# Four graph layers on one core: adjacency and weight products in the array form that TensorE is in, and layer 0's last products by row halves

## The chip, the core and the metric

The kernel runs on one core of a Trainium2 chip. The metric is the time of one execution in microseconds (us) on the device; the runs before the change took 2094.66, 2096.2 and 2099.83 us, a median of 2096.2. A profile is a record of one execution: each instruction of the engines TensorE (PE, with its weight loads as PEld), VectorE (DVE), ScalarE (ACT), GpSimd (POOL) and SyncE (SP), with start and duration.

## What is computed

Eight batches of 2048 nodes with 64 channels go through four layers, each followed by a residual sum and a layer norm. All data is float32.

```python
# layer 0: A is adj (2048 x 2048); emb is 2048 x 16, weight 16 x 3 x 64 x 64
w = einsum('nd,dkio->nkio', emb, weight); b = emb @ bias
x_g = stack([x, A @ x, 2 * A @ (A @ x) - x])
x = layernorm(x + einsum('bnki,nkio->bno', x_g, w) + b)
# layer 1: attention; a is 128 x 1
e = leaky_relu((x @ a[:64]) + (x @ a[64:]).T, 0.2)
att = softmax(where(adj > 0.5, e, -9e15))
x = layernorm(x + elu(att @ x))
# layer 2
x = layernorm(x + (adj + I) @ (x @ W.T + b2) / rowsum(adj + I))
# layer 3: row 0 replaced by a given value, then three steps
for _ in range(3):
    v = relu(concat(v, adj @ v) @ W1.T + b1) @ W2.T + b3
x = layernorm(x + v)
```

## The kernel before

**Data.** The eight batches are taken as four pairs (p = 0 to 3); a pair fills 128 columns (2 batches of 64 channels). SX[p] holds a pair's x as 16 tiles of 128 nodes by 128 columns. SA, SB and SH are three more slots of that size. A chunk (c = 0 to 3) is 512 nodes, four tiles.

**Adjacency products.** `sweep` (L1087) multiplies one or two such sources with the transposed adjacency, which streams from DRAM in tiles of 128 x 2 x 512 (512 KB) over SP's queue into a ring of six. For each chunk, 16 calls (L1106) add up into a PSUM bank `acc` of 128 columns by 512 nodes: weights are a source tile (128 x 128), moving are 512 nodes of adjacency. `sweeps` (L1359) lists all in a fixed order: A x for pairs 0 and 1, then per pair A (A x) together with A x of a later pair, layer 2 and the three steps of layer 3 of pairs 0 and 1, layer 2 of pairs 2 and 3, and last layer 3 of pairs 2 and 3 jointly (`joint_layer3`, L1184, with products at L1219 and L1203). Each whole sweep for one pair has 64 calls, 128 records in the trace, since a call leaves two. Layer 2 of pair 3 waits for `("x2", 3)`, the end of layer 1 for that pair (L1383).

**Layer 0.** `y1_chunk` (L527) takes A x out of PSUM, keeps it node-wise in SA or SB (after transposes, L539) and also writes it to DRAM as `y1_cols`. `stacks` (L559) builds, per chunk, a stack `xgT` of 128 rows for each batch of the pair: 64 rows of x (transposed at L572, two copies) and 64 rows of y1 (one DMA from `y1_cols`). `second_pass` (L584) then makes, for each tile t and each half h of the 16 weight sets, `yp` of 128 nodes x 2 batches x 512: two calls with the 128-row stack and the weights `w01`, one for each batch, and two calls of 64 rows with y2 and `wk2`, in the two row halves of the array (L609). The order is stack first for h = 0, y2 first for h = 1. `add_terms` (L622) weighs the 16 sets by the embedding and adds them into SX on ScalarE and VectorE (L633, L636, L645, L647); `first_norm` (L654) adds the embedding's bias `eb` (L658, on VectorE, from SBUF) and normalises. `embedding_bias` (L376) makes `eb` near the start.

**Layer 1.** `layer1` (L668) transposes x and makes the scores' two halves (L690), `scores` (L709) finds row maxima with the masks (L740), `weights` (L807) makes a tile of exponentials e for both batches: VectorE (L818), ScalarE (L826), VectorE (L831), ScalarE (L834). Two such tiles together go to TensorE at L845: eight calls with 64 columns of weights each, for the two batches in the two column halves of the array, adding up in `po`. Only then is the ring of four e buffers given back. `finish` (L862) ends layer 1 with small products at L879 and a layer norm whose last step is L518.

**Small products.** Also with 128 x 128 weights: L991 (layer 2's weights), L1041 and L1061 (layer 3's), and the seeds of `acc` at L1095. Transposes are at L539, L572, L680, L793 and L1026.

**What sets the order.** The program is scheduled while it is written. Each piece of work is a generator that yields the engine it needs next and what it waits for; `Plan` keeps a clock per engine and in `go` (L99) always continues the piece that could begin first, with a rank where times are equal; sweeps have the lowest rank and fill in. `run` (L69) adds a cost to an engine's clock; `begins` (L89) tells when a piece could begin; `BACK` shifts some pieces by a fixed time; `SLACK` is added to the readiness of TensorE's pieces. The costs are estimates; only the written order reaches the chip, where engines wait for each other by semaphores.

Of the kernel before, what the change touches and what calls it, by code (L numbers as in the profile page):

```python
# [37 lines left out]
class Plan:  # L38
# [7 lines left out]
    SLACK = 0.0  # L46
# [3 lines left out]
        ("add_terms", 0): -3.02,  # L50
        ("finish", None): -0.48,
        ("scores", 2): -0.01,
    }

    def __init__(self):
        self.free = dict.fromkeys(["PE", "DVE", "ACT", "DMA", "SP"], 0.0)
        self.moved = 0.0
        self.at = {}
        self.threads = []
        self.count = itertools.count()  # L60
# [8 lines left out]
    def run(self, eng, cost, *after):  # L69
        t = max([self.free[eng], *(self.when(a) for a in after)]) + cost  # L70
        assert t < NEVER
        self.free[eng] = t
        return t + self.LAG

# [14 lines left out]
    def begins(self, thread):  # L89
        engs, after = thread[3][0:2]  # L90
        ready = max([0.0, *(self.when(a) for a in after)])
        if engs == "PE":
            ready += self.SLACK
        return min(
            (max(self.free[e], ready), i, e)
            for i, e in enumerate((engs,) if isinstance(engs, str) else engs)
        )
# [55 lines left out]
def resnorm_d4_kernel(  # L153
# [116 lines left out]
    w01 = SH[:, 0:8, :].rearrange("p a b -> p (a b)")  # L270
# [19 lines left out]
    def constants():  # L290

        yield "PE", [40.0]
        nc.sync.dma_start(w01, w0[0:P, :])
# [4 lines left out]
        for h in halves:  # L298
            nc.sync.dma_start(wk2[h, :], w0[P : P + C, :])
# [4 lines left out]
        nc.vector.tensor_tensor(w01[0:C, :], w01[0:C, :], wk2[0:C, :], ALU.subtract)  # L304
# [38 lines left out]
    eb = const.tile([P, NT, C], F32, name="eb")  # L343
# [16 lines left out]

    y1_cols = [dram.tile([P, N], F32, name=f"y1_cols{p}") for p in range(NPAIR)]
# [12 lines left out]


    def embedding_bias():  # L376
        yield "PE", [pp_ring]
        pe, k = pp_ring.take([P, NT, C], "ps_eb")
        for t in range(NT):
            nc.tensor.matmul(  # L380
                pe[:, t, :], lhsT=embT[:, t * P : (t + 1) * P], rhs=bias_sb, start=True, stop=True
            )
        done = plan.run("PE", mm(C, NT))
        eng = yield EITHER, [done]
        copy(eng, eb, pe)
        pp_ring.give(k, plan.run(eng, cost(eng, 1024), done))
        e_ring.give(embT_k, plan.free["PE"])

# [43 lines left out]
    def rows_of_adj():  # L432


        for t in range(NT):
            yield "SP", [120.0 + 9.0 * t, bc_ring]
# [3 lines left out]
            done = plan.dma("SP", 1024, bc_ring.t, 120.0 + 9.0 * t)  # L440
            plan.start(1, row_tile(t, an, k, done))
# [117 lines left out]
    def stacks():  # L559

        for n in range(NPAIR * NCH):
            p, c = n // NCH, n % NCH
            yield "DMA", [xg_ring, ("y1T", p, c)]
            xg, kx = xg_ring.take([P, 2, CW], "xgT")
            nc.gpsimd.dma_start(
                xg[C:P], y1_cols[p].rearrange("(e c) n -> c e n", c=C)[:, :, cols(c)]
            )
            got = plan.dma("DMA", 256, xg_ring.t, ("y1T", p, c))
            yield "PE", [pp_ring]
            pt, km = pp_ring.take([P, CW], "ps_xg")  # L570
            for j in range(TPC):
                nc.tensor.transpose(pt[:, j * P : (j + 1) * P], SX[p][:, c * TPC + j, :], ident)  # L572
            t_pe = plan.run("PE", tr(TPC), pp_ring.t)
            for e in range(2):
                eng = yield EITHER, [t_pe]
                copy(eng, xg[0:C, e, :], pt[e * C : (e + 1) * C])
                done = plan.run(eng, cost(eng, CW), t_pe)
            pp_ring.give(km, done)
            stacked.append((xg, kx))
            at["xg", len(stacked)] = max(done, got)  # L580

    stacked = []

    def second_pass():  # L584

        for n in range(NPAIR * NCH):
            yield "PE", [("y2", n + 1), ("xg", n + 1)]
# [3 lines left out]
            for j in range(TPC):  # L591
                t = c * TPC + j
                cs = slice(j * P, (j + 1) * P)
                for h in range(2):
# [5 lines left out]
                    if h == 0 or ring.ready() > plan.free["PE"]:  # L600
                        yield "PE", [("xg", n + 1), got, ring, *([e_ring] if h == 0 else [])]
# [3 lines left out]

                    for k2 in (h, 1 - h):
                        for e in range(2):
                            rows = slice(e * C, (e + 1) * C) if k2 else slice(0, P)
                            nc.tensor.matmul(  # L609
                                yp[:, e, :],  # L610
                                lhsT=y2T[rows, cs] if k2 else xg[:, e, cs],
                                rhs=(wk2 if k2 else w01)[rows, hs],
                                start=(k2 == h),
                                stop=(k2 != h),
                            )
                    t_pe = plan.run("PE", 2.8, got)
# [37 lines left out]
    def first_norm(p, c, done):  # L654
        yield "DVE", [done]
        v = SX[p][:, tiles(c), :]
        v4 = v.rearrange("p t (e c) -> p t e c", c=C)
        nc.vector.tensor_tensor(  # L658
            v4, v4, eb[:, tiles(c), :].unsqueeze(2).to_broadcast([P, TPC, 2, C]), ALU.add
        )  # L660
        done = plan.run("DVE", dve(CW), done)
        done = yield from layer_norm(v, CW, done)
        at["n0", p, c] = done
        if all(("n0", p, i) in at for i in range(NCH)):
            at["x1", p] = max(at["n0", p, i] for i in range(NCH))


    def layer1(p):  # L668
# [7 lines left out]
        for c in range(NCH):  # L676
# [12 lines left out]
            for j in range(TPC):  # L689
                nc.tensor.matmul(  # L690
                    pv[:, j, :], lhsT=xT[:, j * P : (j + 1) * P], rhs=a4, start=True, stop=True
                )
            done = plan.run("PE", mm(4, TPC), got)
# [113 lines left out]
    def weights(p, h, jt, s1b, mb, sv, po, ready):  # L807
# [32 lines left out]
        yield "PE", [("made", p, h, jt - 1), done, *([("weighed", p, h, jt - 2)] if jt > 1 else [])]  # L840
# [12 lines left out]
        done = plan.run("PE", mm(CW, 4) + 0.25, done)  # L853
# [8 lines left out]
    def finish(p, h, po, kpo, xc):  # L862
# [11 lines left out]
        for f in range(2):  # L874
# [3 lines left out]
            for j in range(TPC):  # L878
                nc.tensor.matmul(  # L879
# [6 lines left out]
            t_pe = plan.run("PE", mm(P + 2, TPC), got)  # L886
# [100 lines left out]
    def layer2_tail(p, c, z, kz, done):  # L987
        yield "PE", [done, pp_ring]
        pe, k = pp_ring.take([P, TPC, P], "ps_emb")
        for j in range(TPC):  # L990
            nc.tensor.matmul(  # L991
                pe[:, j, :], lhsT=z[:, j * P : (j + 1) * P], rhs=w2bd, start=True, stop=True
            )
        done = plan.run("PE", mm(P, TPC), done)
        yt_ring.give(kz, done)
        yield "DVE", [done]
# [38 lines left out]
    def u_chunk(p, c, w, dst, bias, s, done):  # L1035

        room = {0: ["y1 used"], 1: ["w0 used"]}.get(s, []) if p == 0 else []
        yield "PE", [done, pp_ring, *room]
        pu, k = pp_ring.take([P, TPC, P], "ps_u")
        for j in range(TPC):  # L1040
            nc.tensor.matmul(  # L1041
                pu[:, j, :], lhsT=SH_of[p][:, c * TPC + j, :], rhs=w, start=True, stop=True
            )
        done = plan.run("PE", mm(P, TPC), done)
# [12 lines left out]
    def last_chunk(p, c, done):  # L1057
        yield "PE", [done, pp_ring]
        pv, k = pp_ring.take([P, TPC, P], "ps_v")
        for j in range(TPC):  # L1060
            nc.tensor.matmul(  # L1061
                pv[:, j, :], lhsT=SH_of[p][:, c * TPC + j, :], rhs=w32c, start=True, stop=True
            )
        done = plan.run("PE", mm(P, TPC), done)
# [12 lines left out]
    def store(p, c, v, done):  # L1077
        yield from layer_norm(v, CW, done, True)
        nc.gpsimd.dma_start(
            out[cols(c), p * P : (p + 1) * P].rearrange("(t p) n -> p t n", p=P), v  # L1080
        )
# [5 lines left out]
    def sweep(*products, masks=False):  # L1087

        for c in range(NCH):
            pas = []  # L1090
            for source, evict, need, before, seed in products:
                yield "PE", [acc_ring, *before(c)]
                pas.append(acc_ring.take([P, CW], "acc"))
                if seed:
                    nc.tensor.matmul(  # L1095
                        pas[-1][0], lhsT=seed[0], rhs=seed[1][:, tiles(c), :], start=True, stop=False
                    )
                    plan.run("PE", mm(CW), *before(c))
            for q in range(AQ):
                n = next(used)  # L1100
                for (source, evict, need, before, seed), (pa, ka) in zip(products, pas):
                    yield "PE", [("a", n), *need(q // 2)]
                    t, k = a_tiles[n]
                    for i in range(2):
                        m = 2 * q + i
                        nc.tensor.matmul(  # L1106
# [6 lines left out]
                    done = plan.run("PE", mm(CW, 2), ("a", n), *need(q // 2))  # L1113
# [325 lines left out]
```

## Time and profile before

| | |
|---|---|
| runs, us | 2094.66, 2096.2, 2099.83 |
| profiled execution, us | 2099.04 |
| its span (first to last instruction), us | 2097.3 |
| TensorE busy, us (share) | 2065.0 (98%), 6325 matmul records |
| VectorE busy, us (share) | 1461.5 (70%) |
| ScalarE busy, us (share) | 989.0 (47%) |
| GpSimd busy, us (share) | 257.6 (12%) |
| granted TensorE clock, mean | 0.995 |
| moved by DMA | 525.22 MB, mean 250 GB/s |
| L1106 on SX, SB, SA, SH: records | 1152, 768, 256, 128 |
| L609 on xgT, on y2T: records | 512, 512 |
| L845: records | 1024 |

Groups of the page read as: line, engine, operation, output<-inputs, shape, count, then busy time (overlaps counted once) and mean time of one. In the timeline of an engine, consecutive records of one kind stand on one line with their common start and the time to the last one's end. Matmul records overlap each other, so what one costs is the distance between two starts.

### The profile page before, as it was taken

To read this page: it belongs to the slowest core of one execution; us is meant where nothing else is said; L and a number is where in the kernel's file an instruction comes from. 1 tells how busy PE (TensorE), PEld (TensorE's weight loads), DVE (VectorE), ACT (ScalarE), POOL (GpSimd) and SP (SyncE) were. 2 spreads that over 40 slices of the span, in tenths; PEclk is the share of its full clock that TensorE was granted. 3 is DMA by queue.
4 is the path that set the end of the run, shared out by engine and by line. 5 is a ranking of instruction groups with operands and counts; after the bars stand their busy time and mean duration, and the time that the engine had idled before them with its cause. 6 is when DMAs were issued, how large, how long until landed. Compare 5 with 4: busy or idle time off the path is not lost.

```text
span 2097.3 us, 19052 instructions
## 1 busy us (share of the span) xinstructions
PE 2065.0 (98%) x6325; PEld 917.1 (44%) x6325; DVE 1461.5 (70%) x1873; ACT 989.0 (47%) x1797; POOL 257.6 (12%) x406
## 2 busy tenths in 40 slices
PE   8999999999999999999999999998999999999997
PEld 3444444444443444444444444443443455444443
DVE  2216756998799999989987979999979732121224
ACT  0014533378877667666266676723757521000002
POOL 2210101211121111112112111001101000000000
PEclk9999999999999999999999999999999999999999
DMA  9798857865475678779969978779787678777785
GB/s 294 257 331 286 299 185 240 277 191 121 130 231 154 161 242 296 235 228 281 336 196 289 286 251 310 245 263 379 226 273 253 217 256 265 268 263 272 265 281 184
DMA packets 221157, 525.22 MB, mean 250 GB/s; under 512 B 21171, under 2 KB 29491, under 8 KB 216691
## 3 DMA queue, kind: packets, MB, share of 16 engines
q1 hardware_dynamic: 170562, 360.20, 51.0%
q0 software_dynamic: 46272, 161.70, 25.1%
q10 hardware_dynamic: 4224, 2.10, 0.4%
q8 instruction: 50, 0.82, 0.2%
q14 instruction: 49, 0.39, 0.1%
HBM read 492.28 MB, written 63.11 MB: 265 GB/s over the span
## 4 chain that ended last, share of the span: by engine, by line
PE 88%; issue 5%; DVE 4%; DMA 2%; ACT 0%; POOL 0%; POOLq 0%; ACTq 0%; DVEq 0%
PE acc L1106 44%; PE yp L609 15%; PE po L845 11%; PE acc L1219 11%; DVE junk L740 2%; PE ps_u L1041 2%; DMA a<-in_adj_t 2%; PE acc L1095 1%; PE acc L1203 1%; DVE terms L645 1%; PE pf L879 1%; PE ps_emb L991 1%; PE ps_sv L690 1%; PE ps_v L1061 0%; PE ps_xT L680 0%
## 5 line engine op out<-in xcount | busy, mean ns | idle before, releaser
L1106 PE MATMUL acc<-a,SX 128*128 128x512 f32 x1152 | 523.7, 600 | 12.5 <-DMA SX<-in_x 6.5
L1106 PE MATMUL acc<-a,SB 128*128 128x512 f32 x768 | 348.6, 597 | 0.4 <-DMA a<-in_adj_t 0.4
L1106 PEld LDWEIGHTS acc<-a,SX 128*128 128x128 f32 x1152 | 214.5, 192 | 276.9 <-issue 259.2
L826 ACT ACTIVATE e<-e,sv 128x1024 f32<-128x1024 f32 x256 | 279.6, 1149 | 80.3 <-DVE e L818 79.5
L633 ACT ACTIVATE terms<-yp,emb_sb 128x128 f32<-128x128 f32 x896 | 243.7, 390 | 130.7 <-PE yp L609 111.9
L831 DVE TENSOR_TENSOR e<-e,mb 128x2048 f32<-128x2048 f32 x128 | 290.4, 2286 | 19.9 <-ACT e L826 19.2
L818 DVE TENSOR_TENSOR e<-s1b,mk 128x2048 f32<-128x2048 f32 x128 | 289.5, 2285 | 8.6 <-PE po L845 7.9
L740 DVE CUSTOM_DVE_ANT_0 junk<-s2b,mr 128x2048 bf16<-128x2048 f32 x128 | 293.0, 2289 | 2.7
L834 ACT ACTIVATE e<-e 128x2048 f32<-128x2048 f32 x128 | 245.0, 1918 | 76.7 <-DVE e L831 76.4
L609 PE MATMUL yp<-SH,xgT 128*128 128x512 f32 x512 | 244.2, 606 | 0.0
L845 PE MATMUL po<-e,SX 128*64 128x512 f32 x1024 | 233.6, 598 | 0.0
L1106 PEld LDWEIGHTS acc<-a,SB 128*128 128x128 f32 x768 | 142.1, 191 | 170.3 <-issue 168.4
L609 PEld LDWEIGHTS yp<-SH,xgT 128*128 128x128 f32 x512 | 90.9, 189 | 137.3 <-issue 131.1
L645 DVE TENSOR_TENSOR terms<-terms 128x512 f32<-128x512 f32 (+1 forms) x176 | 130.0, 739 | 18.5 <-ACT terms L633 14.1
L813 POOL DMA_DIRECT2D mk<-by_col x128 | 71.1, 567 | 518.9 <-DVE e L818 418.3
L845 PEld LDWEIGHTS po<-e,SX 128*64 128x64 f32 x1024 | 67.9, 136 | 147.8 <-issue 135.8
L609 PE MATMUL yp<-SH,y2T 64*128 64x512 f32 x512 | 129.9, 619 | 0.8 <-DVE SB L368 0.8
L1106 PE MATMUL acc<-a,SA 128*128 128x512 f32 x256 | 117.6, 594 | 1.6 <-DMA a<-in_adj_t 1.6
L1219 PE MATMUL acc<-a,t 128*128 128x512 f32 x192 | 85.4, 592 | 0.0
L609 PEld LDWEIGHTS yp<-SH,y2T 64*128 64x128 f32 x512 | 43.2, 185 | 79.6 <-issue 73.7
L636 DVE SCALAR_TENSOR_TENSOR terms<-yp,emb_sb,terms 128x128 f32<-128x128 f32 x128 | 34.6, 344 | 54.8 <-PE yp L609 41.4
L1106 PEld LDWEIGHTS acc<-a,SA 128*128 128x128 f32 x256 | 47.1, 190 | 58.2 <-issue 54.3
(236 smaller groups left out, 1727.0 us busy)
## 6 DMA issues: line engine op xcount, KB each, us to landing
a<-in_adj_t SPq DMA_DIRECT2D x520, 512.0 KB, 5.4
mr<-by_row POOLq DMA_DIRECT2D x64, 512.0 KB, 6.4
mk<-by_col POOLq DMA_DIRECT2D x128, 256.0 KB, 5.6
an<-in_adj SPq DMA_DIRECT2D x16, 1024.0 KB, 11.3
a<-a_plus_i SPq DMA_DIRECT2D x32, 512.0 KB, 5.1
a<-sb SPq DMA_DIRECT2D x24, 512.0 KB, 4.4
a<-sc SPq DMA_DIRECT2D x24, 512.0 KB, 4.3
a<-sd SPq DMA_DIRECT2D x24, 512.0 KB, 4.5
```

The source lines that it names most:

```text
L609: nc.tensor.matmul(yp[:, e, :], lhsT=y2T[rows, cs] if k2 else xg[:, e, cs], rhs=(wk2 if k2 else w01)[rows, hs], start=(k2 == h), stop=(k2 ...
L633: nc.scalar.activation(batches(terms[0][:, dd, :]), term, AF.Copy, scale=weight)
L645: nc.vector.tensor_tensor(a, a, b, ALU.add)
L740: nc.vector.tensor_tensor_reduce(out=junk, in0=s2b[e][0], in1=masks[t][0], scale=1.0, scalar=LOWEST, op0=ALU.add, op1=ALU.max, accum_out=m ...
L813: nc.gpsimd.dma_start(mk, by_col[jt // 2][:, jt % 2, h * HALF : (h + 1) * HALF])
L818: nc.vector.tensor_tensor(e, s1b[0], mk.unsqueeze(1).to_broadcast([P, 2, HALF]), ALU.add)
L826: nc.scalar.activation(e[:, i, :], e[:, i, :], AF.Prelu, bias=sv[:, 2 + i, jt : jt + 1], alpha=ALPHA)
L831: nc.vector.tensor_tensor(e, e, mb[0], ALU.add)
L834: nc.scalar.activation(e, e, AF.Exp)
L845: nc.tensor.matmul(po[i * C : (i + 1) * C, f, :], lhsT=SX[p][:, t, i * C : (i + 1) * C], rhs=e[:, i, f * CW : (f + 1) * CW], start=(t == 0 ...
L1106: nc.tensor.matmul(pa, lhsT=source[:, m, :], rhs=t[:, i, :], start=(m == 0 and not seed), stop=(m == NT - 1),)
L1219: nc.tensor.matmul(pa, lhsT=B[:, 2 * r + b, :], rhs=at_[:, b, :], start=(start and r == 0 and b == 0), stop=(r == RQ - 1 and b == 1), skip ...
```

## The change

- A matmul has a form: the whole array ("PE"), row halves ("PE rows") or column halves ("PE columns"). The plan keeps the form that TensorE was last in, charges 0.2 us for each change of it, and delays a piece that would change it to rows or columns by `HOLD` 0.5; `SLACK` becomes 0.3.
- Adjacency products, their seeds in `sweep`, and the small products at L690, L879, L991, L1041 and L1061 take the form "PE any", through a new helper `multiply`: where the last form was column halves they are written as two calls with 64 columns of weights each, into the two halves of the output's partitions; else as one call.
- Layer 0's last products are three pairs of calls by row halves: x with `wk0`, y1 with `wk1`, y2 with `wk2`, each with the two batches in the two halves. `xgT` holds x and y1 side by side instead of stacked: one copy of 128 partitions and one DMA of 128 partitions.
- `wk1` takes the place in SBUF that `eb` had. `eb` is written to DRAM, twice side by side, and added to each chunk of SX by an accumulating DMA on GpSimd's queue, after the chunk's transposes and A x are done; the second pass of that chunk is planned after it. The addition at L658 goes.
- `w0` is loaded in six parts instead of three; rows of adj are fetched from 130 us on, 9.5 us apart, instead of 120 and 9.0; the planned costs of L609 and L845 lose their extra; `BACK` has other entries; two waits on stored chunks are written out.

```diff
-    SLACK = 0.0
+    SLACK = 0.3
+    FORMS = ("PE", "PE rows", "PE columns", "PE any")
+    SWITCH = 0.2
+    HOLD = 0.5
...
     BACK = {
-        ("add_terms", 0): -3.02,
-        ("finish", None): -0.48,
-        ("scores", 2): -0.01,
+        ("add_terms", 0): -0.03,
+        ("add_terms", 1): -0.11,
+        ("add_terms", 2): -0.13,
+        ("greatest", None): -1.14,
+        ("out_of", None): 0.95,
+        ("row_tile", None): -1.44,
+        ("scores", 0): -1.14,
+        ("start_chunk", None): -0.37,
+        ("sums", None): 5.39,
     }
...
     def run(self, eng, cost, *after):
+        if eng in self.FORMS:
+            if eng == "PE any":
+                eng = self.either()
+            if eng != self.form:
+                cost += self.SWITCH
+            self.form, eng = eng, "PE"
...
+    def either(self):
+        return "PE" if self.form == "PE rows" else self.form
...
-        if engs == "PE":
-            ready += self.SLACK
+        if engs in self.FORMS:
+            hold = self.HOLD if engs not in (self.form, "PE") else 0.0
+            return (max(self.free["PE"], ready + self.SLACK + hold), 0, engs)
...
+    def multiply(out, lhsT, rhs, **kw):
+        halves = (slice(0, C), slice(C, P))
+        for h in halves if plan.either() == "PE columns" else (slice(0, P),):
+            nc.tensor.matmul(out[h], lhsT=lhsT[:, h], rhs=rhs, skip_group_check=True, **kw)
...
-            nc.gpsimd.dma_start(
-                xg[C:P], y1_cols[p].rearrange("(e c) n -> c e n", c=C)[:, :, cols(c)]
-            )
+            nc.gpsimd.dma_start(xg[:, 1, :], y1_cols[p][:, cols(c)])
...
-            for e in range(2):
-                eng = yield EITHER, [t_pe]
-                copy(eng, xg[0:C, e, :], pt[e * C : (e + 1) * C])
-                done = plan.run(eng, cost(eng, CW), t_pe)
+            plan.start(1, add_eb(p, c, t_pe))
+            eng = yield EITHER, [t_pe]
+            copy(eng, xg[:, 0, :], pt)
+            done = plan.run(eng, cost(eng, CW), t_pe)
...
+    def add_eb(p, c, done):
+        yield "DMA", [done, ("y1T", p, NCH - 1), "eb"]
+        nc.gpsimd.dma_start(
+            SX[p][:, tiles(c), :],
+            eb[:, tiles(c), :, :].rearrange("p t e c -> p t (e c)"),
+            accum_op=ALU.add,
+        )
+        at["eb", p, c] = plan.dma("DMA", 450, done, ("y1T", p, NCH - 1), "eb") + 0.5
...
-                    for k2 in (h, 1 - h):
+                    for k3, (v, w) in enumerate(((xg[:, 0], wk0), (xg[:, 1], wk1), (y2T, wk2))):
                         for e in range(2):
-                            rows = slice(e * C, (e + 1) * C) if k2 else slice(0, P)
+                            rows = slice(e * C, (e + 1) * C)
                             nc.tensor.matmul(
                                 yp[:, e, :],
-                                lhsT=y2T[rows, cs] if k2 else xg[:, e, cs],
-                                rhs=(wk2 if k2 else w01)[rows, hs],
-                                start=(k2 == h),
-                                stop=(k2 != h),
+                                lhsT=v[rows, cs],
+                                rhs=w[rows, hs],
+                                start=(k3 == 0),
+                                stop=(k3 == 2),
                             )
-                    t_pe = plan.run("PE", 2.8, got)
+                    t_pe = plan.run("PE rows", mm(CW, 3), got)
...
-        nc.vector.tensor_tensor(
-            v4, v4, eb[:, tiles(c), :].unsqueeze(2).to_broadcast([P, TPC, 2, C]), ALU.add
-        )
...
-        done = plan.run("PE", mm(CW, 4) + 0.25, done)
+        done = plan.run("PE columns", mm(CW, 4), done)
...
-                        nc.tensor.matmul(
+                        multiply(
                             pa,
                             lhsT=source[:, m, :],
                             rhs=t[:, i, :],
                             start=(m == 0 and not seed),
                             stop=(m == NT - 1),
                         )
-                    done = plan.run("PE", mm(CW, 2), ("a", n), *need(q // 2))
+                    done = plan.run("PE any", mm(CW, 2), ("a", n), *need(q // 2))
```

More of the change, by code (lines that the diff above doesn't have):

```diff
@@ L59, in __init__ @@
         self.threads = []
+        self.form = "PE"
         self.count = itertools.count()
@@ L269, in resnorm_d4_kernel @@
         fetch(n)
-    w01 = SH[:, 0:8, :].rearrange("p a b -> p (a b)")
+    wk0 = SH[:, 0:8, :].rearrange("p a b -> p (a b)")
     wk2 = SH[:, 8:16, :].rearrange("p a b -> p (a b)")
@@ L292, in constants @@
         yield "PE", [40.0]
-        nc.sync.dma_start(w01, w0[0:P, :])
         nc.sync.dma_start(emb_sb, emb.rearrange("(t p) d -> p t d", p=P))
@@ L297, in constants @@
         halves = [slice(0, C), slice(C, P)]
-        for h in halves:
-            nc.sync.dma_start(wk2[h, :], w0[P : P + C, :])
+        for k, w in enumerate((wk0, wk1, wk2)):
+            for h in halves:
+                nc.sync.dma_start(w[h, :], w0[k * C : (k + 1) * C, :])
         for k in range(2):
@@ L303, in constants @@
         yield "PE", [70.0]
-        nc.vector.tensor_tensor(w01[0:C, :], w01[0:C, :], wk2[0:C, :], ALU.subtract)
+        nc.vector.tensor_tensor(wk0, wk0, wk2, ALU.subtract)
         nc.vector.tensor_scalar_mul(wk2, wk2, 2.0)
@@ L342, in resnorm_d4_kernel @@
     rdeg = const.tile([P, NT], F32, name="rdeg")
-    eb = const.tile([P, NT, C], F32, name="eb")
+    wk1 = const.tile([P, D0 * C], F32, name="wk1")
     gv = const.tile([P, P], F32, name="gv")
@@ L359, in resnorm_d4_kernel @@
     }
+    eb = dram.tile([P, NT, 2, C], F32, name="eb")
     y1_cols = [dram.tile([P, N], F32, name=f"y1_cols{p}") for p in range(NPAIR)]
@@ L383, in embedding_bias @@
         done = plan.run("PE", mm(C, NT))
-        eng = yield EITHER, [done]
-        copy(eng, eb, pe)
-        pp_ring.give(k, plan.run(eng, cost(eng, 1024), done))
-        e_ring.give(embT_k, plan.free["PE"])
+        eng = yield EITHER, [done, e_ring]
+        sb, ke = e_ring.take([P, NT, C], "eb_sb")
+        copy(eng, sb, pe)
+        done = plan.run(eng, cost(eng, 1024), done)
+        pp_ring.give(k, done)
+        e_ring.give(embT_k, plan.free["PE"])
+        for e in range(2):
+            nc.gpsimd.dma_start(eb[:, :, e, :], sb)
+            done = plan.dma("DMA", 512, done)
+        e_ring.give(ke, done)
+        at["eb"] = done
     def weights_of_l23():
@@ L435, in rows_of_adj @@
         for t in range(NT):
-            yield "SP", [120.0 + 9.0 * t, bc_ring]
+            yield "SP", [130.0 + 9.5 * t, bc_ring]
             an, k = bc_ring.take([P, 2, HALF], "an")
@@ L439, in rows_of_adj @@
             nc.sync.dma_start(an, adj[t * P : (t + 1) * P, :])
-            done = plan.dma("SP", 1024, bc_ring.t, 120.0 + 9.0 * t)
+            done = plan.dma("SP", 1024, bc_ring.t, 130.0 + 9.5 * t)
             plan.start(1, row_tile(t, an, k, done))
@@ L586, in second_pass @@
         for n in range(NPAIR * NCH):
-            yield "PE", [("y2", n + 1), ("xg", n + 1)]
+            yield "PE rows", [("y2", n + 1), ("xg", n + 1), ("eb", n // NCH, n % NCH)]
             p, c, y2T, ky, got = queue[n]
@@ L600, in second_pass @@
                     if h == 0 or ring.ready() > plan.free["PE"]:
-                        yield "PE", [("xg", n + 1), got, ring, *([e_ring] if h == 0 else [])]
+                        yield "PE rows", [("xg", n + 1), got, ring, *([e_ring] if h == 0 else [])]
                     if h == 0:
@@ L654, in first_norm @@
     def first_norm(p, c, done):
-        yield "DVE", [done]
-        v = SX[p][:, tiles(c), :]
-        v4 = v.rearrange("p t (e c) -> p t e c", c=C)
-        nc.vector.tensor_tensor(
-            v4, v4, eb[:, tiles(c), :].unsqueeze(2).to_broadcast([P, TPC, 2, C]), ALU.add
-        )
-        done = plan.run("DVE", dve(CW), done)
-        done = yield from layer_norm(v, CW, done)
+        done = yield from layer_norm(SX[p][:, tiles(c), :], CW, done)
         at["n0", p, c] = done
@@ L689, in layer1 @@
             for j in range(TPC):
-                nc.tensor.matmul(
+                multiply(
                     pv[:, j, :], lhsT=xT[:, j * P : (j + 1) * P], rhs=a4, start=True, stop=True
                 )
-            done = plan.run("PE", mm(4, TPC), got)
+            done = plan.run("PE any", mm(4, TPC), got)
             xt_ring.give(kx, done)
@@ L839, in weights @@
             return
-        yield "PE", [("made", p, h, jt - 1), done, *([("weighed", p, h, jt - 2)] if jt > 1 else [])]
+        yield "PE columns", [("made", p, h, jt - 1), done, *([("weighed", p, h, jt - 2)] if jt > 1 else [])]
         mine = [held.pop((p, h, t)) for t in (jt - 1, jt)]
@@ L878, in finish @@
             for j in range(TPC):
-                nc.tensor.matmul(
+                multiply(
                     pp[:, j, 0 : P + 2],
@@ L885, in finish @@
                 )
-            t_pe = plan.run("PE", mm(P + 2, TPC), got)
+            t_pe = plan.run("PE any", mm(P + 2, TPC), got)
             if f == 1:
@@ L990, in layer2_tail @@
         for j in range(TPC):
-            nc.tensor.matmul(
+            multiply(
                 pe[:, j, :], lhsT=z[:, j * P : (j + 1) * P], rhs=w2bd, start=True, stop=True
             )
-        done = plan.run("PE", mm(P, TPC), done)
+        done = plan.run("PE any", mm(P, TPC), done)
         yt_ring.give(kz, done)
-        yield "DVE", [done]
+        yield "DVE", [done, *([("stored", 1, c)] if p == NPAIR - 1 else [])]
         v = after_l2(p)[:, tiles(c), :]
@@ L1035, in u_chunk @@
     def u_chunk(p, c, w, dst, bias, s, done):
-        room = {0: ["y1 used"], 1: ["w0 used"]}.get(s, []) if p == 0 else []
+        room = {(0, 0): ["y1 used"], (0, 1): ["w0 used"], (2, 0): [("stored", 0, c)]}.get((p, s), [])
         yield "PE", [done, pp_ring, *room]
@@ L1040, in u_chunk @@
         for j in range(TPC):
-            nc.tensor.matmul(
+            multiply(
                 pu[:, j, :], lhsT=SH_of[p][:, c * TPC + j, :], rhs=w, start=True, stop=True
             )
-        done = plan.run("PE", mm(P, TPC), done)
+        done = plan.run("PE any", mm(P, TPC), done)
         if bias is None:
@@ L1060, in last_chunk @@
         for j in range(TPC):
-            nc.tensor.matmul(
+            multiply(
                 pv[:, j, :], lhsT=SH_of[p][:, c * TPC + j, :], rhs=w32c, start=True, stop=True
             )
-        done = plan.run("PE", mm(P, TPC), done)
+        done = plan.run("PE any", mm(P, TPC), done)
         at["spent", p, c] = done
@@ L1078, in store @@
         yield from layer_norm(v, CW, done, True)
+        at["stored", p, c] = 0.0
         nc.gpsimd.dma_start(
@@ L1094, in sweep @@
                 if seed:
-                    nc.tensor.matmul(
+                    multiply(
                         pas[-1][0], lhsT=seed[0], rhs=seed[1][:, tiles(c), :], start=True, stop=False
                     )
-                    plan.run("PE", mm(CW), *before(c))
+                    plan.run("PE any", mm(CW), *before(c))
             for q in range(AQ):
@@ L1105, in sweep @@
                         m = 2 * q + i
-                        nc.tensor.matmul(
+                        multiply(
                             pa,
```

## The prediction, made before any run of the changed kernel

> **What bounds the kernel now.** I read the head of the page first, then its chain of the work that ended last.
>
> ```profile
> span 2097.3 us, 19052 instructions
> ...
> PE 2065.0 (98%) x6325; PEld 917.1 (44%) x6325; DVE 1461.5 (70%) x1873; ACT 989.0 (47%) x1797; POOL 257.6 (12%) x406
> ...
> PE 88%; issue 5%; DVE 4%; DMA 2%; ACT 0%; POOL 0%; POOLq 0%; ACTq 0%; DVEq 0%
> ```
>
> TensorE is busy from end to end and is 88% of the chain, at a granted clock of 0.995. But busy time hides what a matmul costs, because matmuls overlap. The timeline of TensorE shows it by the distance from start to start. One visit of layer 0's last products, between adjacency products, at 1010 us:
>
> ```profile
> 1009.82 1.98 PE L1106 MATMUL acc<-a,SB 128*128 128x512 f32 x4 [0.36 <-DMA a<-in_adj_t]
> 1011.64 1.88 PE L609 MATMUL yp<-SH,xgT 128*128 128x512 f32 x4
> 1013.45 1.99 PE L609 MATMUL yp<-SH,y2T 64*128 64x512 f32 x8
> 1015.37 1.98 PE L609 MATMUL yp<-SH,xgT 128*128 128x512 f32 x4
> 1017.19 3.60 PE L1106 MATMUL acc<-a,SB 128*128 128x512 f32 x8
> 1020.62 0.27 PE L793 MATMUL ps_rows<-ident,mx 128*16 128x128 f32 x1
> ```
>
> The columns are start, time, instruction, count of records (a call leaves two). Undisturbed, eight records take 1020.62 - 1017.19 = 3.43 us: 0.429 each. The four xgT records before the y2T ones take 1013.45 - 1011.64 = 1.81, not 1.72: 0.09 more. The eight y2T records use half the rows, run two at a time and take 1.92, not 1.72: 0.20 more, about 0.10 on entering and 0.10 on leaving. The next four take 1.82: 0.10 more. So **an excursion from the whole array to row halves and back costs 0.39 us** (four parts, in ns: 93, 104, 90, 104). The same reading for layer 1's weighted sums, which use column halves:
>
> ```profile
> 799.16 2.31 PE L1106 MATMUL acc<-a,SX 128*128 128x512 f32 x5
> 801.40 3.65 PE L845 MATMUL po<-e,SX 128*64 128x512 f32 x16
> 804.99 3.70 PE L1106 MATMUL acc<-a,SX 128*128 128x512 f32 x8
> 808.53 0.72 PE L991 MATMUL ps_emb<-w2bd,z 128*128 128x128 f32 x5
> ```
>
> Sixteen records in eight pairs take 3.59 for 3.43, the eight after them 3.54 for 3.43; with 0.09 ahead this is **0.34 us for an excursion into column halves**. Both forms stream at full rate in between: a pair costs what one whole record costs.
>
> Then I counted, in the whole timeline of TensorE, where one record's form differs from the next one's: 73 excursions into rows and 63 into columns, 272 switches. Price: 73 x 0.393 + 63 x 0.343 = 50.3 us (28.7 and 21.6 by summing each switch's own excess). The span then adds up: 6.5 before the first matmul, 2000 of streaming, 50.3 of switches, some 31 of waits and of matmuls at half speed after a wait (DMA in the first 150 us, 4 us at 290, 6.5 near 1441), 9.9 after the last start.
>
> **A second bound** stands beside TensorE. The sweep of layer 2 for pair 3 needs all of layer 1 for that pair, which VectorE makes. The lines of VectorE and TensorE at that place:
>
> ```profile
> 1684.18 0.69 DVE L518 TENSOR_TENSOR SX<-SX,ln_r 128x512 f32<-128x512 f32 x1
> ```
> ```profile
> 1688.02 1.05 PE L1041 MATMUL ps_u<-w31e,SH 128*128 128x128 f32 x8
> 1688.91 1.88 PE L1106 MATMUL acc<-a,SX 128*128 128x512 f32 x4
> ```
>
> Layer 1 ends at 1684.9 and the sweep begins at 1688.9 (counted back 128 records from the joint layer 3). VectorE has only 4 us in hand. All switches lie before that point, and from there to the end is 408.4 us with nothing that the change touches. So time = 408.4 + the later of two arrivals.
>
> **The change, part by part.**
>
> *Streaming.* Half a tile of layer 0's last product takes now two whole calls and a pair of row halves; after, three pairs of row halves (x, y1, y2 apart). Both are 3 x 0.858: 0. An adjacency product in column halves is a pair of calls, each with half of the weights' columns. L845 is the row for it: 0.429 per pair of records, 0. L845 feeds its halves different data and the products the same; I know of no row where that matters.
>
> *Small products* (L690, L879, L991, L1041, L1061: 896 records) may also run as column pairs. No row has a short pair. From above: the halves run one after the other, 0.112 more for each record so split, 304 by the count below, 34 us. From below: L690 moves 4 columns and still takes 0.112, so it waits for its weights; two half loads at once could save half of it, 128 x 0.056 = 7 us. I take 0, as in L845 the second of a pair starts 6 to 7 ns after the first.
>
> *Switches.* I went through the records in their present order with the new rule: L609 all rows, L845 columns, the transposes whole, and the rest whichever form is set (whole after rows). 142 switches are left: 51 into rows and 51 out of them, 43 to whole and 8 straight to columns; 30 entries into columns in all, 18 exits to whole. At 0.197 into rows, 0.196 and 0.198 to whole, 0.144 into columns that is 10.0 + 8.4 + 4.3 + 3.6 = 26.3 us, so **24.0 us less**. Bounds: 0 (the new order breaks every run) and 50.3 (none left). TensorE would reach pair 3's sweep at 1688.9 - 24.0 = 1664.9.
>
> *VectorE.* Gone are sixteen additions of eb at 0.684 (10.9 us), and of 32 half copies into xgT (8 on VectorE at 0.688, 24 on ScalarE at 0.578) one of two: 2.8 and 6.9. VectorE is busy 1220 of the 1345 us from 340 to 1685, so work taken off it moves layer 1 forward almost in full: 13.7. Its waits for TensorE in that stretch are 61.5 us (26.1 of them at L891); an earlier TensorE takes some away. I take 5, a choice between 0 and 61.5, low since the written order fixes most of them. Layer 1 ends at 1684.9 - 18.7 = 1666.2.
>
> *New DMAs.* eb goes to DRAM and is added to SX by sixteen accumulating DMAs of 256 KB on POOL's queue. The nearest rows: accumulating 512 KB lands after 10.0 us (sc<-in_adj_t), a plain 256 KB after 4.4 (xgT<-y_cols), and the issue takes up to 1.14 on POOL. They may start when the chunk is transposed (L572), and pair 0's also when y1 is complete (134 us). From L572 to the first addition into that SX chunk (L647) lie 48 us or more; pair 0 has 159 - 134 = 25. Hidden; without that cover each costs up to 10. Queued behind one on POOL are mask loads, so its 16 x 1.14 us of issue could hold VectorE; POOL is busy 12%: 0. Three more loads of w0 on SP, which also feeds the adjacency, add 0.5 MB, under 2 us at 289 GB/s in the first 150 us. rows_of_adj starts 10 us later, away from two waits of TensorE for adjacency (0.85 and 0.77 at 140): 0 net, +-3.
>
> *SLACK and HOLD.* A TensorE step is planned 0.3 us after its input, and 0.5 more if it would switch. Nothing runs longer; the written order shifts, and with it which waits are met. No row prices it; the bounds are the third rival and the gain of the waits above.
>
> *Sum.* The later arrival is layer 1's, 1666.2, plus 0.3 for the hand-over: 1666.5 + 408.4 = 2074.9 of span. The profiled execution took 2099.0 for its 2097.3, so 2076.6; it lay 2.8 above the median 2096.2. I say **2075**.
>
> **A rule against it.** The row first: in L845's groups the weight loads of both column halves begin right behind the matmul before them and the pairs keep 0.429. The Trainium skill (TensorE: Matmul & The Clock Gate, Part 3, What overlaps and what doesn't) says that weight loads overlap running matmuls only where the row group differs; column halves share theirs. By it, 940 adjacency records in column form would each expose a load, L845's 0.136, so +128 us and about 2200. The row decides against that rule.
>
> **Rivals.**
> 1. *VectorE binds.* The chain of layer 1 gets little of the 13.7, as the eb additions lie before 1091 and pair 3's scores begin only at 1318. Then TensorE waits at pair 3's sweep: 1685 + 408.4 is 2093 to 2096 with nothing gained, 2085 with half. For it: 4 us in hand. Against: VectorE is busy without much gap since 340. 0.25.
> 2. *It does more.* The planner gathers the forms, about 80 switches are left (15 us), and waits near 290 and 1441 fall with the new order (10): 2097 - 35 - 10 and layer 1 as early: 2050 to 2063. Against: VectorE must gain 45. 0.13.
> 3. *Slower: the hold makes column work late.* L845 gives back the e buffers, of which four exist. If a group waits the hold and then behind an adjacency step (1.72), 16 groups of pair 3 delay VectorE by 27 us, and layer 1 ends at 1693 or later even after the 18.7: 2102 to 2120. It decides once VectorE loses more than some 23 us on L845; now it loses 7.9 in all. 0.12.
> 4. *It does not do what it says*: transposes and row visits break the column runs, 200 switches stay, 14 us gained: about 2085, inside the forecast's reach.
>
> **How the numbers follow.** The forecast, 2063 to 2088, with rival 4: 0.50. Rival 1 is 0.25, of which 0.11 is still faster by over 0.3% (below 2089.9; 0.3% is what a measurement here tells from no change) and 0.14 within it; rival 2 is 0.13, rival 3 0.12, of it 0.02 within. So faster 0.74, same 0.16, slower 0.10. The range takes in rival 1 and half of rival 2, and the costs unknown by a few us: 2054 to 2099.
>
> **What would show it.** TensorE's timeline: about 140 changes of form, L609 all 64*128, L1106 partly 128*64 with pairs 0.429 apart. L658 gone from VectorE. A wait of TensorE ahead of pair 3's first L1106 means rival 1, one of VectorE's L818 on L845 rival 3. I am wrong at the root if pairs of L1106 stand over 0.45 apart.

## The result, and the profile after

The changed kernel takes 2084.29 us (median of 4 runs, 2081.43 to 2086.10) against 2098.01 (4 runs: the three listed ahead and 2101.46): a ratio of 0.993 with a 95% interval of 0.9918 to 0.9943. It is faster by 13.7 us; the profiled executions, 2081.43 and 2099.04, stand 17.6 apart. The head of the page after:

```profile
span 2079.5 us, 22115 instructions
...
PE 2042.8 (98%) x7845; PEld 889.4 (43%) x7845; DVE 1441.2 (69%) x1847; ACT 981.1 (47%) x1791; POOL 267.2 (13%) x424
...
PE 86%; issue 5%; DMA 4%; DVE 3%; ACT 1%; SPq 0%; POOL 0%; POOLq 0%; DVEq 0%; ACTq 0%
```

TensorE is still busy end to end, with 1520 matmul records more than before: 1008 from pairs of column halves where one call was, 512 from layer 0's row halves. The shares moved little; what moved shows in TensorE's timeline, read again by distances from start to start (L405 is the new helper, L884 the weighted sums):

```profile
1289.66 3.17 PE L405 MATMUL acc<-a,SX 128*64 128x512 f32 x14
1292.66 1.04 PE L405 MATMUL ps_emb<-w2bd,z 128*64 128x128 f32 x16
1293.53 3.60 PE L884 MATMUL po<-e,SX 128*64 128x512 f32 x16
1296.97 7.04 PE L405 MATMUL acc<-a,SX 128*64 128x512 f32 x32
1303.83 3.60 PE L884 MATMUL po<-e,SX 128*64 128x512 f32 x16
...
1316.61 3.65 PE L884 MATMUL po<-e,SX 128*64 128x512 f32 x16
1320.09 7.04 PE L405 MATMUL acc<-a,SX 128*64 128x512 f32 x32
```

In the first five lines TensorE never leaves column halves. The weighted sums take 1296.97 - 1293.53 = 3.44 us, eight pairs at 0.43 with nothing added; before they took 3.59 with more on either side. The 32 records of the product are 16 pairs and take 6.86: also 0.43. The small product ps_emb takes 0.87 for eight pairs, 0.109 each, where a whole record took 0.112. A transpose at 1307.37 has put TensorE back to the whole array, where the products behind it stay; so the sums at 1316.61 take 3.48: the switch is back. The longest stretch in column halves has 736 records, from 1501 to 1633 us.

Row halves, at 936 us (the middle of the visit left out):

```profile
933.95 1.98 PE L405 MATMUL acc<-a,SB 128*128 128x512 f32 x4
935.86 1.13 PE L655 MATMUL yp<-SH,xgT 64*128 64x512 f32 x4
...
940.26 1.02 PE L655 MATMUL yp<-SH,y2T 64*128 64x512 f32 x4
941.21 7.13 PE L405 MATMUL acc<-a,SB 128*128 128x512 f32 x16
```

The visit is all 64*128: 941.21 - 935.86 = 5.35 for twelve pairs, which undisturbed take 5.15: one excursion for the whole visit.

I took both timelines apart as the prediction did: each distance between two starts less 0.429 us (0.109 to 0.112 for short matmuls) is a switch if the form changes there or just did, and otherwise a wait or the half speed that follows one.

| us of the span | before | after |
|---|---|---|
| ahead of the first matmul, behind the last start | 16.4 | 15.8 |
| streaming | 2004.7 | 2003.0 |
| switches (number) | 50.3 (272) | 28.4 (158) |
| waits, and half speed after them | 25.7 | 32.1 |

The rows add up to the span but for 0.2 us; the prediction's 2000 of streaming and 31 of waits divide the same sum a little differently. So 21.9 us of switches went, and 6.4 of it came back as waits.

### The profile page after: what moved, and what is told of

It reads as the page before. It is cut to its first block, busy times and chain, and to the rows that moved or that the text cites. A ratio compares the mean times of both kernels' runs of the same rounds, so it can differ in the third digit from the quotient of the medians.

```text
span 2079.5 us, 22115 instructions
## 1 busy us (share of the span) xinstructions
PE 2042.8 (98%) x7845; PEld 889.4 (43%) x7845; DVE 1441.2 (69%) x1847; ACT 981.1 (47%) x1791; POOL 267.2 (13%) x424
## 4 chain that ended last, share of the span: by engine, by line
PE 86%; issue 5%; DMA 4%; DVE 3%; ACT 1%; SPq 0%; POOL 0%; POOLq 0%; DVEq 0%; ACTq 0%
PE acc L405 45%; PE yp L655 14%; PE acc L1260 10%; PE po L884 10%; DMA a<-in_adj_t 3%; PE ps_u L405 2%; DVE junk L779 1%; DVE terms L691 1%; PE acc L1244 1%; PE ps_emb L405 1%; PE pf L405 1%; ACT terms L679 1%; PE ps_sv L405 1%; ACT e L865 0%; DVE e L857 0%
## 5 line engine op out<-in xcount | busy, mean ns | idle before, releaser
L405 PE MATMUL acc<-a,SX 128*128 128x512 f32 (+1 forms) x1544 | 521.4, 596 | 7.9 <-DMA SX<-in_x 6.6
L405 PE MATMUL acc<-a,SB 128*128 128x512 f32 (+1 forms) x1000 | 354.7, 598 | 6.5 <-DMA a<-in_adj_t 5.8
L405 PEld LDWEIGHTS acc<-a,SX 128*128 128x128 f32 (+1 forms) x1544 | 196.5, 164 | 281.5 <-issue 270.3
L679 ACT ACTIVATE terms<-yp,emb_sb 128x128 f32<-128x128 f32 x896 | 242.4, 394 | 133.8 <-PE yp L655 133.4
L884 PE MATMUL po<-e,SX 128*64 128x512 f32 x1024 | 231.6, 595 | 0.0
L405 PEld LDWEIGHTS acc<-a,SB 128*128 128x128 f32 (+1 forms) x1000 | 130.5, 166 | 189.8 <-issue 176.4
L655 PE MATMUL yp<-SH,xgT 64*128 64x512 f32 x512 | 138.5, 618 | 5.6 <-ACT terms L679 4.8
L655 PE MATMUL yp<-wk,xgT 64*128 64x512 f32 x512 | 132.0, 592 | 0.0
L884 PEld LDWEIGHTS po<-e,SX 128*64 128x64 f32 x1024 | 70.6, 137 | 143.3 <-issue 133.9
L405 PE MATMUL acc<-a,SA 128*128 128x512 f32 (+1 forms) x288 | 119.0, 597 | 2.7 <-DMA a<-in_adj_t 2.7
L655 PEld LDWEIGHTS yp<-SH,xgT 64*128 64x128 f32 x512 | 44.5, 187 | 79.2 <-issue 64.9
L655 PEld LDWEIGHTS yp<-wk,xgT 64*128 64x128 f32 x512 | 49.9, 188 | 60.8 <-issue 60.6
L655 PEld LDWEIGHTS yp<-SH,y2T 64*128 64x128 f32 x512 | 49.8, 188 | 60.7 <-issue 60.7
```

The source lines that it names most:

```text
L405: nc.tensor.matmul(out[h], lhsT=lhsT[:, h], rhs=rhs, skip_group_check=True, **kw)
L655: nc.tensor.matmul(yp[:, e, :], lhsT=v[rows, cs], rhs=w[rows, hs], start=(k3 == 0), stop=(k3 == 2),)
L679: nc.scalar.activation(batches(terms[0][:, dd, :]), term, AF.Copy, scale=weight)
L884: nc.tensor.matmul(po[i * C : (i + 1) * C, f, :], lhsT=SX[p][:, t, i * C : (i + 1) * C], rhs=e[:, i, f * CW : (f + 1) * CW], start=(t == 0 ...
```

## The experiments

Each is compared with the kernel before, run beside it on the same chip, with 95% intervals; switches and waits are taken from each one's profile as above.

| run | ratio to before | median us | switches us (number) | waits us | span us |
|---|---|---|---|---|---|
| before | | 2098 to 2100 | 50.3 (272) | 25.7 | 2097.3 |
| after | 0.993 (0.9918 to 0.9943) | 2084.3 | 28.4 (158) | 32.1 | 2079.5 |
| e1_whole | 0.9984 (0.9972 to 0.9997) | 2096.8 | 41.6 (230) | 31.3 | 2092.7 |
| e2_flip | 1.0298 (1.028 to 1.0316) | 2162.0 | 114.2 (670) | 31.1 | 2164.6 |
| e3_no_eb | 0.9999 (0.9988 to 1.001) | 2098.7 | 50.3 (272) | 25.5 | 2096.1 |
| e4_hold0 | 0.9985 (0.9974 to 0.9997) | 2097.2 | 30.6 (171) | 41.6 | 2091.4 |
| e5_old_settings | 0.9912 (0.9897 to 0.9927) | 2083.0 | 27.3 (151) | 34.7 | 2081.2 |
| e6_new_settings | 1.005 (1.0034 to 1.0066) | 2110.9 | 50.3 (273) | 38.5 | 2109.5 |
| e7_rows_only | 0.9987 (0.9977 to 0.9998) | 2097.2 | 40.8 (227) | 35.1 | 2095.4 |
| e8_rows_early | 0.9882 (0.9868 to 0.9896) | 2074.7 | 28.9 (160) | 25.7 | 2075.1 |
| e9_no_cols_rows_early | 0.9953 (0.9936 to 0.997) | 2090.0 | 41.3 (229) | 26.1 | 2086.2 |
| e10_hold0_rows_early | 0.9929 (0.9916 to 0.9942) | 2085.5 | 28.8 (161) | 39.2 | 2087.4 |

Subtract switches and waits from the span: 2018.8 to 2021.3 is left in all twelve. A kernel of this family is 2020 us plus its switches plus its waits, and each run can be read by these two columns. This is an account of each trace, since the rest is matmuls at a fixed price; what shows the cause is e1 and e2, which change the forms and nothing of the order.

**e1_whole: the column form alone, taken back in the same order.**

```diff
-        for h in halves if plan.either() == "PE columns" else (slice(0, P),):
+        for h in (slice(0, P),):
```

> The changed kernel in the very order that was written for it, but each product that may choose its form is issued as one call on the whole array (1741 calls on the whole array become 2245, column calls 1524 become 516). Counted in the written order, 44 more switches out of columns to whole and 30 more into columns: 44 x 0.198 + 30 x 0.144 = 13.0 us more. Theory (TensorE's switches are the time): 2084.3 + 13 = 2097, and the streaming of 2002 us unchanged. Rival (the gain came from elsewhere, the column form of the products is worth nothing or costs something): 2084 or below.

Measured 2096.8; the switches cost 41.6 us, 13.2 more than after. The same place in its timeline, with the order unchanged:

```profile
1302.40 3.65 PE L884 MATMUL po<-e,SX 128*64 128x512 f32 x16
1305.98 7.13 PE L405 MATMUL acc<-a,SX 128*128 128x512 f32 x16
1313.05 3.65 PE L884 MATMUL po<-e,SX 128*64 128x512 f32 x16
```

3.58 and 7.07 where after has 3.44 and 6.86. With the order fixed, the column form of the products is worth 12.5 us at the medians, 11.3 by the two ratios to before (whose intervals do not meet) and 13.2 in the profiles: nearly all of the change's 13.7. The other 8.7 us of switches, 50.3 less 41.6, are those of the row halves and the new order, and in e1 waits eat 5.6 of them (31.3 for 25.7).

**e2_flip: four times the switches.**

```diff
+    flips = itertools.cycle((True, False))
...
-        for h in halves if plan.either() == "PE columns" else (slice(0, P),):
+        for h in halves if (plan.either() == "PE columns" if split is None else split) else (slice(0, P),):
...
+                    split = next(flips)
                     for i in range(2):
...
+                            split=split,
```

> The changed kernel in the very order that was written for it, but each step of two adjacency calls takes the other array form than the step before it, whole or column halves in turn. Some 500 switches more between whole and columns (177 become 676 in the written order), at a mean of 0.171 us. Theory (a switch costs its drain and its uncovered weight load, and nothing hides it): 2084 + 85 = 2169. Rival (switches overlap with what follows, or the form of the products matters by itself): less than half of that, below 2127.

Measured 2162.0; in the profile 512 switches more cost 85.8 us, 0.168 each, and the waits stay (31.1). By the medians it is 77.7 us slower than after, by the spans 85.1. The added switches cost on average what the prediction had read (0.171), so nothing hides them.

**e3_no_eb: work off VectorE alone.** The addition at L658 is left out, so layer 0 lacks its bias; the order is that of before.

```diff
-        nc.vector.tensor_tensor(
-            v4, v4, eb[:, tiles(c), :].unsqueeze(2).to_broadcast([P, TPC, 2, C]), ALU.add
-        )
```

> The kernel before with its written order unchanged, but without the sixteen additions of the embedding's bias on VectorE (L658); the bias of layer 0 is left out of the result. That takes 10.9 us off VectorE and nothing off TensorE. Theory (TensorE alone sets the time, VectorE has room before pair 3's sweep): 2098, within 0.2%. Rival (VectorE's layer 1 sets when pair 3's sweep begins): faster by 5 to 11 us.

0.9999: VectorE's 10.9 us were worth nothing. The end of layer 1 of pair 3, and the sweep's first product:

```profile
1682.99 0.69 DVE L518 TENSOR_TENSOR SX<-SX,ln_r 128x512 f32<-128x512 f32 x1
```
```profile
1687.72 1.88 PE L1102 MATMUL acc<-a,SX 128*128 128x512 f32 x4
```

Layer 1 ended at 1683.7 instead of 1684.9, and the sweep began at 1687.7 instead of 1688.9: of 10.9 us taken off VectorE, layer 1 moved by 1.2.

**e7_rows_only: all but the column form.**

```diff
     def either(self):
-        return "PE" if self.form == "PE rows" else self.form
+        return "PE"
```

> The changed kernel with layer 0 by row halves and the bias by DMA, but no product in column halves; the planner knows it and writes its own order. 242 switches in the written order, 65 more than the changed kernel, about 0.171 each: 11 us. Theory: 2095, so that row halves, bias by DMA and the planner's settings alone are worth some 3 us. Rival (the gain is that of the planner's settings or of VectorE's relief): 2084.

Measured 2097.2, some 2 us better than before, though its switches cost 9.5 us less: the waits grew by 9.4.

**Where the waits come from.** In after the longest behind the start begins at 244 us. ScalarE's and TensorE's timelines there:

```profile
229.98 0.23 ACT L393 COPY sv<-ps_sv 128x16 f32<-128x16 f32 x1
242.81 1.91 ACT L485 ACTIVATE an<-an 128x2048 f32<-128x2048 f32 x1 [12.60 <-DMA an<-in_adj]
244.63 0.19 ACT L485 ACTIVATION_READ_ACCUMULATOR an<-an 128x1 f32 x1
245.35 1.91 ACT L485 ACTIVATE an<-an 128x2048 f32<-128x2048 f32 x1 [0.54 <-DMA an<-in_adj]
247.17 0.19 ACT L485 ACTIVATION_READ_ACCUMULATOR an<-an 128x1 f32 x1
247.26 4.21 ACT L679 ACTIVATE terms<-yp,emb_sb 128x128 f32<-128x128 f32 x16
```
```profile
240.99 3.70 PE L405 MATMUL acc<-a,SA 128*128 128x512 f32 x8
249.47 2.08 PE L655 MATMUL yp<-SH,xgT 64*128 64x512 f32 x4 [4.78 <-ACT terms L679]
251.33 1.77 PE L655 MATMUL yp<-wk,xgT 64*128 64x512 f32 x4
252.94 1.02 PE L655 MATMUL yp<-SH,y2T 64*128 64x512 f32 x4
```

ScalarE stands 12.6 us before a row of adj that has not landed (L485, the row sums). The terms at L679 are written behind it, and only they give TensorE its PSUM buffers back; so TensorE waits 4.8 us, and its next four pairs, up to 252.94, take 3.47 us instead of 1.72, 1.75 more. The granted clock is 0.52 in these 3.47 us and 1.00 in the 4 us behind them.

**e8_rows_early: rows fetched closer together, and planned to land later.**

```diff
-            yield "SP", [130.0 + 9.5 * t, bc_ring]
+            yield "SP", [130.0 + 8.5 * t, bc_ring]
...
-            plan.start(1, row_tile(t, an, k, done))
+            plan.start(1, row_tile(t, an, k, done + 8.0))
```

> The changed kernel with the rows of adj fetched 8.5 us apart instead of 9.5, and planned to land 8 us later than before, so that ScalarE's work on a row (L485) is written behind other work until the row is surely there. 179 switches, 2 more. Theory (at 244 us ScalarE stands behind a row that has not landed, the terms behind it, and TensorE behind those: 4.8 us, and 1.9 more at half speed after it): that wait goes, 2084 - 6 = 2078. Rival (the wait only moves, as the PSUM buffers are short in that stretch): 2083 to 2085.

2074.7, faster than both kernels. ScalarE's timeline now:

```profile
235.08 2.18 ACT L679 ACTIVATE terms<-yp,emb_sb 128x128 f32<-128x128 f32 x8 [2.97 <-PE yp L655]
...
245.28 2.18 ACT L679 ACTIVATE terms<-yp,emb_sb 128x128 f32<-128x128 f32 x8 [2.60 <-PE yp L655]
249.13 1.91 ACT L485 ACTIVATE an<-an 128x2048 f32<-128x2048 f32 x1 [1.67 <-DMA an<-in_adj]
```

The row comes behind the terms, the wait is gone (6.6 us of waits from 150 to 260 us become 0), and all waits together are 25.7, as many as before the change. Two things were changed at once, the rows' times and the place of ScalarE's work, and the order is a new one; which of them did it is not told apart. Between the medians lie 9.6 us, between the profiled spans 4.4, as that of after was its fastest execution and that of e8 its slowest.

**e9_no_cols_rows_early: the same mend on e7.** Its edits are those of e7 and e8 together.

> The kernel of e7 (row halves, bias by DMA, new settings, no product in column halves) with the same earlier rows as e8. e7 has 52 switches fewer than the kernel before, worth 9 us, but is only some 2 us faster, and its waits grew by 9 us. Theory (the wait on ScalarE near 247 us took most of what row halves gained): 2097 - 6 = 2091. Rival (the row halves cost something else): 2096 to 2098.

2090.0, and waits fall from 35.1 to 26.1. Against before it has 9.0 us less of switches and 0.4 more of waits, and is 0.5% faster, some 10 us. So the switches that row halves save show in the time once this wait does not eat them; bias by DMA and the settings are in this run too.

**e6_new_settings: the settings alone, on the kernel before** (BACK, SLACK and the rows' times as after).

> The kernel before with nothing of the change but the planner's settings: BACK, SLACK 0.3, rows of adj from 130 us on, 9.5 apart. 299 switches in the written order, 5 more than before: 1 us. Theory (settings alone give nothing; the gain is in the switches): 2099 to 2101, unless waits move by some us. Rival (the settings, which end layer 1 of pair 3 some 40 us earlier, are worth part of the gain): 2090 or less.

2110.9, slower by 0.5%: no switch less, and 12.8 us more waits, most from TensorE waiting for terms twice near 203 and 249 us. Both theories missed. The settings do not make the gain; on the kernel before they cost. Layer 1 of pair 3 ended at 1641.3, 43.6 us earlier than before, and pair 3's sweep began at 1701.2, 12.3 later: an early layer 1 is worth nothing by itself.

**e5_old_settings: the change with the settings of before** (old BACK, SLACK 0, HOLD 0, old times of the rows).

> The changed kernel with the planner's settings of before: BACK, SLACK 0, HOLD 0 and the rows of adj from 120 us on, 9.0 apart. 171 switches in the written order, 6 fewer than the changed kernel. Theory A (the column form and nothing else makes the gain, VectorE has room anyway): 2083. Theory B (with the old settings layer 1 of pair 3 ends near 1685 less some 14 us of relief, as before, and a faster TensorE must wait there): a wait of TensorE ahead of the first adjacency product of pair 3's layer 2, and 1671 to 1685 + 408 + 2 = 2081 to 2095. The wait in the trace tells them apart, not the time alone.

2083.0, the same as after. The end of layer 1 of pair 3 on VectorE, and the sweep's first product on TensorE:

```profile
1668.89 0.69 DVE L551 TENSOR_TENSOR SX<-SX,ln_r 128x512 f32<-128x512 f32 x1
```
```profile
1673.61 1.88 PE L399 MATMUL acc<-a,SX 128*128 128x512 f32 x4
```

No wait, and 4.0 us between the end (1669.6) and the start: as before, and as in e3. Theory B had layer 1's end nearly right (1671), but its wait is not there: layer 1 moved 15.3 us ahead, as much as TensorE did.

**e4_hold0 and e10_hold0_rows_early.** The edit is `HOLD = 0.0` in after and in e8.

> The changed kernel with HOLD 0 instead of 0.5, so that a piece that switches TensorE's form is not put off; the planner writes another order, with 190 switches instead of 177. Theory (switches and waits of TensorE make the time): 13 x 0.17 = 2 us more, 2086, give or take 6 for other waits. Rival 3 of the prediction (the hold makes column work late and VectorE lose time): VectorE's waits on the weighted sums fall, layer 1 of pair 3 ends earlier, and the kernel is faster, 2078 or less.

> HOLD 0 as in e4, with the rows of adj as in e8. 180 switches, 1 more than e8. Theory (what HOLD 0 lost in e4, 13 us, was the same wait for ScalarE near 245 us and other waits that the order happens to meet, not the switches): about 2078, e8's 2075 and a few us. Rival (without HOLD the order is worse in itself): 2085 or more.

2097.2 and 2085.5: both slower by 11 to 13 than their pairs, with 2 us and nothing more of switches, and with 9.5 and 13.5 us more of waits. e4 waits 6.7 us for the terms where after waits 4.8; e10 waits mainly for adjacency tiles (15.3 us in all, e8 7.9). Neither theory of e4 holds; e10's is missed by 7, and its rival's 2085 is met. But e5 has HOLD 0 as well, with the old settings and rows' times, and is as fast as after; so these runs do not show that HOLD 0 is worse in itself. Why these two orders meet more waits is not settled; that they do is what the columns show.

## Why the prediction was right or wrong

**Switches: right.** 24.0 us were forecast with 142 left; 21.9 went with 158 left, and e1 and e2 price a switch at 0.183 (13.2 us for 72) and 0.168. The order of before was a good enough stand-in for the order after. By e1, 13.2 us of it belong to the column form and 8.7 to the row halves and the new order.

**Streaming, small products, and to trust L845's row over the rule against it: right.** Pairs of L405 stand 0.43 apart, short pairs 0.109 to 0.111. Products whose two halves read the same data cost no more than L884's, whose halves differ.

**The accumulating DMAs: hidden, as said.** They land after a median of 7.6 us (4.1 to 15.8; two of the sixteen took longer than the 10 that the prediction set as the most); no wait in the trace is put down to them.

**The second bound: wrong, and it is the step that failed.** "VectorE has only 4 us in hand", "work taken off it moves layer 1 forward almost in full" and "time = 408.4 + the later of two arrivals" took two events that stand close together for a race. In the order of before they were one chain. The lines of before that say so were on VectorE, just ahead of the one I showed, and on TensorE:

```profile
1664.06 0.21 DVE L891 RECIPROCAL rd<-pf 128x8 f32<-128x8 f32 x1 [2.81 <-PE pf L879]
...
1674.87 0.21 DVE L891 RECIPROCAL rd<-pf 128x8 f32<-128x8 f32 x1 [1.99 <-PE pf L879]
```
```profile
1673.78 1.06 PE L879 MATMUL pf<-back,poT 128*128 128x130 f32 x8
```

VectorE's last two pieces of layer 1 both waited for TensorE. What follows the second takes 10 us, and TensorE has 14 us of other work queued behind L879, which leaves the 4. Hence in e3 layer 1 moved by 1.2 us and not by 10.9, and in e5, where the last piece still waited 0.31 for TensorE, both moved by 15.3. In after the two are far apart:

```profile
1639.84 0.69 DVE L557 TENSOR_TENSOR SX<-SX,ln_r 128x512 f32<-128x512 f32 x1
```
```profile
1668.36 5.32 PE L405 MATMUL acc<-a,SX 128*128 128x512 f32 x12
```

Layer 1 ends at 1640.5, 25.7 earlier than forecast, and TensorE comes at 1671.8 (the last four of these records are pair 3's), 6.9 later. So layer 1 was no bound. What moved its end this far are the settings, which the prediction left without a price: e6 has them without the rest of the change and ends layer 1 at 1641.3, e5 has the rest without them and ends it at 1669.6. The sum, with layer 1 as the later arrival at 1666.2, landed near the span (2074.9 against 2079.5) by the wrong term: TensorE's own path, at 1664.9, stood 1.3 from it. That closeness is luck; TensorE's path was the right term, and it was too short by the waits below and by 2.1 of switches.

**Rivals 1, 2 and 4.** Rival 1 fell with the second bound: TensorE does not wait ahead of pair 3's sweep. Rival 2's 80 changes of form were 158. Its condition, that VectorE gain 45 us, was met (layer 1 ended 44.4 earlier) and brought nothing. Rival 4's time, about 2085 with 14 us gained, is the measured one, but not for its reason: it had 200 changes left and 14 us of switches gained, where 21.9 were gained and 6.4 lost to waits.

**Waits: mis-sized.** New DMAs and settings were taken as 0 net. The two waits at 288 to 299 and near 431 us went, 7.1 of 260 to 460 us becoming 0.6; new are the one on ScalarE (6.6), 2.3 more from 460 to 760 us and 1.5 from 760 to 900, and 2.7 more near 1395, where TensorE waits for adjacency. Net, with small ones elsewhere, +6.4: with 2.1 fewer of switches, and 2.3 gained in streaming and at the ends of the span, 24 became 17.8. The wait near 1395 belongs to a moment that before and e8 have too, when layer 1's first half for pair 3 starts:

```profile
1380.00:1410.00 30.00, 25.21 (x56) 10.06 (x56) 28.64 (x21) 7.25 (x7) 6.64 (x12) 0.89 1.02 387
```

The columns are the window, its length, then busy time (records) of TensorE, its weight loads, VectorE, ScalarE and GpSimd, granted clock, DMA share and GB/s: the DMA engines are full, TensorE idles and its clock falls. In before, the stretch from 1425 to 1455 us has a DMA share of 1.04 and TensorE busy for 23.99, and there the clock stays at 1.00.

**Rival 3: refuted.** VectorE waits 1.5 us for the weighted sums in the 340 to 1685 us stretch, where it waited 7.9. In e4 and e10 the lack of HOLD comes with other waits and a slower kernel, in e5 with neither.

**The rest.** The forecast of 2075 is 9.3 below the median: 4.6 in the span, 1.6 that the prediction took off its 2076.6, 2.9 because the profiled execution was the fastest of its four and lies that far under their median, and 0.2 between span and execution. The slower ones, 2083.9 and 2084.2 of span, have a granted clock of 0.993 instead of 0.995. That fits more waits, but no trace of them shows which; it stays open.

## What to carry to other kernels

Where TensorE is busy from end to end, read its cost by distances from start to start: a change between the whole array and halves shows there as some 0.17 us a time, in no busy total. If one form cannot be avoided, bring the neighbours into it; a 128 x 128 product in two column halves streams as fast as whole. Two engines that arrive together need not race: look what the later pieces of the one waited for before calling it a bound, and look what stands behind an in-order wait, since here a late row on ScalarE cost TensorE as much as 40 switches.

## What the runs showed that I had not expected

What a wait of TensorE costs beyond itself is a matter of the granted clock, and it is not fixed. After the 4.8 us at 244 four pairs take 3.47 us instead of 1.72 at a clock of 0.52, and then they stand 0.43 apart again. But the wait of 2.1 us at 553 us in after is followed by a clock of 1.00, and the same wait in e8, at 549 us, by one of 0.53 over 3.6 us. What decides it is not shown. And the written order's luck is nearly as large as the change: at equal switches (160 and 161), e8 and e10 differ by 10.8 us.
